# The first quad's layer-0 aggregation as seven block products, with the beginning in another order

## The chip, the cores and the metric

The kernel runs on one core of a Trainium2 chip. TensorE (PE) multiplies into PSUM, VectorE (DVE), ScalarE (ACT) and GpSimd (POOL) work on SBUF and PSUM, and SyncE (SP) issues every DMA of this kernel on one queue. The metric is the device time of one execution in microseconds: the median of three runs, 1771.18 us (1770.94 to 1771.25).

## The reference, cut to what matters

```python
# x: (16, 1024, 128) float32, adj: (1024, 1024) float32
h = relu(layernorm(x))                     # layer 0
x = x + (adj @ (h @ weight) + bias)
h = relu(layernorm(x))                     # layer 1: five gated steps
for _ in range(5):
    m = adj @ h                            # both matrices of the step are adj
    z = sigmoid(m @ w3 + h @ u3 + b3)      # w3 stands for the sum of its two halves
    r = sigmoid(m @ w4 + h @ u3 + b4)
    hv = tanh(m @ w5 + (r * h) @ u5 + b5)
    h = (1 - z) * h + z * hv
x = x + h
```

Everything is float32. Nearly all the arithmetic is `adj @ h`: once per batch in layer 0 and five times in layer 1.

## The kernel before, in words

The 16 batches are worked in four quads of four. One aggregation multiplies the adjacency matrix with the hidden states of a whole quad. In layer 1 it is done with Strassen's scheme in Winograd's form at two levels: seven big products, each again of seven small ones (`aggregate`, L502). The right operands of the small products are blocks of the transposed adjacency matrix and their sums and differences. They never change, so they are worked out once at the beginning (`right_sums`), written to DRAM tiles called `rd` (nine of the 49 stay in SBUF, `RESIDENT`), and read again for every aggregation in the fixed order `STREAM`, pair by pair, into `ring`, which has seven places for a pair (`stream`).

Layer 0 of the first two quads is done in the beginning, straight from the raw adjacency tiles. This document calls the aggregation of the first quad stage A and that of the second stage B.

- **Stage A** (`aggregate_plainly`, L549, names `pq_a0`): for each of two column halves of the adjacency matrix and each of four batches, eight matmuls of 128x128 by 128x512 into one PSUM bank, then a copy to `mT`. That is 64 matmuls.
- **Stage B** (`aggregate_by_seven`, L618, names `a_a1`, `b_a1`, `c_a1`): one level of the scheme. The left operand is a 2x2 matrix of blocks (two batches by two halves of the nodes), the right one the raw adjacency matrix in 2x2 blocks. Seven products p, each for two batches, each of four matmuls: 56 matmuls. Products 1, 2 and 3 take raw blocks; products 5, 6, 7 and 4 take differences T1, T2, T3 and T4 of raw blocks on the right, and sums S1 to S4 of the states on the left.
- After an aggregation, `po` (L741) multiplies `mT` with the layer's weight, four matmuls of 128x128 for each batch and half, and DVE adds the result to `x`.

The order is written out by hand. `pin` keeps each instruction in program order on its engine, so every engine is a queue. `put(k, ...)` hangs pieces on place k of the running aggregation, and `place(k)` issues them there, in the order in which they were put. In stage A before, k counts half rows of eight matmuls; in `aggregate_by_seven` k counts half-products (one product for one batch), 1 to 14.

Around the two stages lie these pieces:

- The loads. The adjacency matrix comes in eight tiles `raw[i][g]` of 512 KB (i: two chunks of 128 rows, g: column half). The g = 0 tiles lie in `big`, the others in `Z` and `little`. `x` comes in 512 KB a batch. `other_loads(k)` groups the loads behind the first ones; a memset of one column by DVE ahead of a group makes its first DMA wait until DVE has come that far, and SP, which issues in order, holds the rest.
- `Norm`, the layer norm of a batch: `bn_stats` (L330) on each of eight chunks, `bn_aggr` (L339), `ve` (L341) on DVE; the power -1/2 on POOL (L342, `rstd`); the shift on DVE (L347, `nmr`); eight `relu` activations on ACT (L360).
- The right sums. The big ones are T1 to T4, two differences of 128x1024 each, which lie in the ring's room until the ring is loaded for the first time. The small ones, for each of the seven big products in two halves: half 0 stores three blocks as they are and two computed ones, half 1 two more. Those in `RESIDENT` aren't stored. Each computed block is a 128x512 difference on DVE, and each store a DMA of 256 KB on SP's queue.
- In stage B, layer 1's input of the first quad is prepared: norm, `park` (four DMAs of 128 KB, `ft<-nat`), `store_x1` (one of 512 KB), then the load of the second quad's `x` into the same tile, and the transposing loads `sqt<-ft`. At its end stand seven `stream()` calls, which fill the ring for step 0, the first layer-1 aggregation.

Of the kernel before, what the change touches and what calls it, by code (L numbers as in the profile page):

```python
# [8 lines left out]
F32 = mybir.dt.float32  # L9
# [4 lines left out]
P = 128  # L14
# [82 lines left out]
def tile_two_gnn_layers(  # L97
# [36 lines left out]
    def x_tile(b):  # L134
        return pre.tile([P, NC, D], F32, tag="xt", name=f"xt_{b}")

    def load_x(b, xt=None, parts=((0, NC),)):
        xt = xt if xt is not None else x_tile(b)
        for cs in parts:
            cs = slice(*cs)  # L140
            dma(xt[:, cs], by_slots(x[b])[:, cs])
        return xt
# [23 lines left out]
    def flat(t):  # L166
        names = "abcd"[: len(t.shape) - 1]
        return t.rearrange(f"p {' '.join(names)} -> p ({' '.join(names)})")
# [7 lines left out]
    def load_adj(i, g):  # L176
        parts = SB if (i, g) == (0, 0) else 1
        for k in range(parts):
            cs = bass.ts(k, SB // parts)
            dma(raw[i][g][:, cs], adjT[:, bass.ts(i, SB), bass.ts(g, HALF)][:, cs])  # L180

    xts = {0: load_x(0, parts=((0, 2), (2, CH), (CH, NC)))}
    xts.update({b: x_tile(b) for b in range(1, Q)})
    for i in range(2):
        load_adj(i, 0)

    early_x = {}

    def other_loads(k):
        if k == 0:
            pin(nc.vector.memset(xts[1][:, 0, 0:1], 0.0))
            load_x(1, xts[1])
            load_adj(2, 0)
        elif k == 1:
            pin(nc.vector.memset(raw[3][0][:, 0, 0:1], 0.0))
            load_adj(3, 0)
        else:
            pin(nc.vector.memset(xts[2][:, 0, 0:1], 0.0))  # L200
            for b in range(2, Q):
                load_x(b, xts[b])
            for i in range(NB):
                load_adj(i, 1)
            for b in range(Q, Q + 3):
                early(b)
            dma(gb, gbias.to_broadcast([P, D]))
            dma(w_sb, weights)
            dma(b_sb, biases)
# [30 lines left out]

    def right_sums():

        rooms = [flat(ring[:, 4 * k : 4 * k + 4]) for k in range(3)]
        count = [0]

        def big_sum(n):
            room = rooms[{1: 2, 2: 0, 3: 1, 4: 2}[n]]
            T[n] = [room[:, bass.ts(k, N)].rearrange("p (c n) -> p c n", c=SB) for k in range(2)]
            for k in range(2):
                R = {(a, b): raw[2 * (a - 1) + k][b - 1] for a in (1, 2) for b in (1, 2)}  # L250
                a, b = {
                    1: (R[1, 2], R[1, 1]),
                    2: (R[2, 2], T.get(1, [0, 0])[k]),
                    3: (R[2, 2], R[1, 2]),
                    4: (R[2, 1], T.get(2, [0, 0])[k]),
                }[n]
                sub(T[n][k], a, b)

        def target(key):
            if key in RESIDENT:  # L260
# [23 lines left out]
                store_right((i, 4), t4)  # L284
                store_right((i, 7), t3)

        steps = [lambda n=n: big_sum(n) for n in (1, 2, 3)]
        steps += [lambda i=i, h=h: small_sums(i, h) for i in (3, 2, 0, 4, 1, 5) for h in range(2)]
        steps += [lambda: big_sum(4)]
        steps += [lambda h=h: small_sums(6, h) for h in range(2)]  # L290
        return steps

    streamed = [0]

# [243 lines left out]
                piece()  # L538
            place(k + 1)

    def aggregate_plainly(hN, nm, place):

        k = 0
        for g in range(NH):
            for i in range(Q):
                bank = ps_g.tile([P, HALF], F32, tag="pg", name=f"pq_{nm}_{i}_{g}")
                for c in range(NC):
                    pin(
                        nc.tensor.matmul(  # L549
                            bank,  # L550
                            hN[i][:, c, :],
                            raw[c // SB][g][:, c % SB],
                            start=c == 0,
                            stop=c == NC - 1,
                        )
                    )
                    if c == CH - 1:
                        k += 1
                        place(k)
                pin(nc.scalar.copy(mT[:, i, bass.ts(g, HALF)], bank))  # L560
                k += 1
                place(k)

    def aggregate_by_seven(hN, nm, place):

        S = {}
        for n in (2, 1, 3):
            t = flip.tile([P, 2, CH, D], F32, tag="sq", name=f"S{n}_{nm}")
            S[n] = [t[:, i] for i in range(2)]
        S[4] = []  # L570
        for i in range(2):
            t = work.tile([P, HALF], F32, tag="hv", name=f"S4{i}_{nm}", bufs=3)
            S[4].append(t.rearrange("p (j d) -> p j d", j=CH))

        def part(a, b, i):
            return hN[2 * a + i][:, bass.ts(b, CH)]

        def left_sums(n):
            for i in range(2):
                op, x, y = {  # L580
                    1: (add, part(1, 0, i), part(1, 1, i)),
                    2: (sub, S[1][i], part(0, 0, i)),
                    3: (sub, part(0, 0, i), part(1, 0, i)),
                    4: (sub, part(0, 1, i), S[2][i]),
                }[n]
                op(S[n][i], x, y)

        def result(a, b, i):
            return mT[:, 2 * a + i, bass.ts(b, HALF)]

        left_sums(1)
        left_sums(2)
        banks, fifth = {}, {}
        k = 0
        for p in BIG:
            right = big_right(BIG.index(p)) if p in (1, 2, 3) else T[{5: 1, 6: 2, 7: 3, 4: 4}[p]]
            for i in range(2):
                left = {
# [17 lines left out]
                for c in range(CH):  # L616
# [7 lines left out]
                            skip_group_check=True,  # L624
                        )
                    )
                if p == 2:
                    add(result(0, 0, i), bank, result(0, 0, i))
                elif p == 3:
                    add(result(0, 1, i), bank, result(0, 1, i))  # L630
                elif p == 5:
                    fifth[i] = work.tile([P, HALF], F32, tag="z", name=f"P5{i}_{nm}")
                    pin(nc.scalar.copy(fifth[i], bank))
                else:
                    o = {1: result(0, 0, i), 6: result(0, 1, i), 7: result(1, 1, i), 4: result(1, 0, i)}[p]
                    pin(nc.scalar.copy(o, bank))
                    if p == 7:
                        add(o, o, fifth[i])
                k += 1
                if k in (3, 4):  # L640
                    left_sums(k)
                place(k)


    def scratch_for(kind, nm):

# [465 lines left out]
    firsts = [slotwise(nat[:, k]) for k in range(Q)]  # L1112
    seconds = [slotwise(hT_all[:, 1, k].rearrange("p (a j e) -> p a j e", a=NSQ, e=SQ)) for k in range(Q)]

    one, two = Norm(xts[0], firsts[0][1], "a0"), Norm(xts[1], firsts[1][1], "a1")
    parts = (range(2), range(2, CH), range(CH, NC))
    for k in range(2):
        one.statistics(parts[k])
        one.scales(parts[k])
        if k == 0:  # L1120
            other_loads(0)
    one.shift(parts[0])
    one.relu(parts[0])
    one.statistics(parts[2])
    one.scales(parts[2])
    other_loads(1)
    one.shift(parts[1])
    one.relu(parts[1])
    one.shift(parts[2])
    one.relu(parts[2])  # L1130
    two.statistics(range(CH))
    other_loads(2)
    two.statistics(range(CH, NC))
    two.scales(EVERY)
    two.shift(EVERY)
    two.relu(EVERY)

    sums = right_sums()

# [1 line left out]
        for _ in range(n):  # L1141
            put(k, sums.pop(0))

    def norm_at(k, src, dst, nm, done=None, now=None):

        box = {}

        def begin():
            box["n"] = Norm(src(), dst, nm)
            box["n"].statistics(EVERY)  # L1150
            box["n"].scales(EVERY)

        def rest():
            box["n"].shift(EVERY)
            box["n"].relu(EVERY)
            if done:
                done()

        put(k, begin)
        if now is not None:  # L1160
            sums_at(k, now)
        put(k + 1 if now is None else k, rest)

    norm_at(1, lambda: xts[2], firsts[2][1], "a2")
    norm_at(2, lambda: xts[3], firsts[3][1], "a3", now=0)
    sums_at(3, 1)
    for b, k in zip(range(Q, 2 * Q), (4, 5, 6, 8)):
        done = (lambda: early(2 * Q - 1)) if b == Q else None
        norm_at(k, lambda b=b: early_x[b], seconds[b - Q][1], f"a{b}", done, 1)
    for b in range(Q):  # L1170
        put(8 + b, lambda b=b: bias(b))
    for k in (7, *range(9, 16)):
        sums_at(k, 1)
    for b in range(Q):
        put(11 + b, lambda b=b: po(b, 0))
    put(15, lambda: po(0, 1))
    put(16, lambda: po(1, 1))
    aggregate_plainly([s for s, _ in firsts], "a0", place)

    put(1, lambda: po(2, 1))  # L1180
    put(2, lambda: po(3, 1))

    def first_done(b):
        park(b, nat[:, b])
# [5 lines left out]
    for b in range(Q):  # L1190
        norm_at(2 * b + 1, lambda b=b: xts[b], nat[:, b], f"b{b}", lambda b=b: first_done(b))
        put((3, 5, 7, 10)[b], lambda b=b: xts.update({Q + b: load_x(Q + b)}))
        put((6, 8, 10, 14)[b], lambda b=b: bias(Q + b))
    for k in (2, 4, 8, 9, 10):
        sums_at(k, 1)
    put(7, weight_sums)
    for b, g, k in ((0, 0, 7), (1, 0, 9), (2, 1, 11), (0, 1, 13), (1, 1, 13), (3, 1, 14)):
# [5 lines left out]
    put(12, *early_0[2:6])  # L1203
    put(13, *early_0[6:8])
    put(14, *early_0[8:10])
    aggregate_by_seven([s for s, _ in seconds], "a1", place)
    for _ in range(RING // 2):
        stream()
    for b in range(2):
# [66 lines left out]
```

## Time and profile before

| what | value |
|---|---|
| median of three timed runs | 1771.18 us |
| span of the profiled execution | 1768.8 us |
| TensorE busy | 1759.3 us, 99% of the span |
| DVE busy | 1375.7 us |
| ACT busy | 899.0 us |
| mean granted TensorE clock | 0.999 |
| DMA moved | 396.88 MB, 224 GB/s over the span |
| stage A, first to last matmul's successor | 5.48 to 69.43 us |
| stage B, to the first product of step 0 | 69.43 to 126.43 us |

The page gives no other time for the profiled execution than its span; the timed runs' median is 2.4 us longer. In the lines of a timeline the first number is the start in microseconds from the span's start, the second the length of the merged group, then the engine, the line of the kernel, the operation, the tiles written and read, and the number of instructions; in brackets stands how long the engine was idle before, and what ended that wait. A line of a table by stretch gives the stretch, its length, the busy microseconds and instructions of PE, PEld (the weight load), DVE, ACT and POOL, then the granted clock, the mean busy share of the 16 DMA engines and the GB/s that they moved.

### The profile page before, as it was taken

The numbers are of one execution on the slowest core, as the hardware profiler recorded it, in microseconds if no ns is written. First come the engines' busy times: TensorE is split into PE (matmuls) and PEld (weight loads), VectorE is DVE, ScalarE is ACT, GpSimd is POOL, SyncE is SP. The second block draws the span as 40 slices with busy tenths as digits, with TensorE's granted clock in tenths as the row PEclk, the third lists the DMA queues.
The fourth block names the chain that finished last, engine by engine and source line by source line (L and its number), as shares of the span: only waits on it lengthen the run. The fifth ranks groups of instructions, "written<-read, shape, count | busy, mean of one in ns | idle before, by whom it ended". The sixth has DMA issues, their size and how long they took to land.

```text
span 1768.8 us, 21424 instructions
## 1 busy us (share of the span) xinstructions
PE 1759.3 (99%) x6438; PEld 1200.6 (68%) x6438; DVE 1375.7 (78%) x2806; ACT 899.0 (51%) x1974; POOL 59.0 (3%) x41
## 2 busy tenths in 40 slices
PE   9999999999999999999999999999999999999998
PEld 3557667589585775858857667585775857667584
DVE  6778988777878687887687968777687777868787
ACT  5246556544555555554455554545455454545544
POOL 3101000000000000000000000000000000000000
PEclk9999999999999999999999999999999999999999
DMA  7499786578595956749849577594866749476684
GB/s 258 157 324 306 235 257 214 179 240 250 129 305 185 284 198 195 236 135 284 241 146 326 176 227 279 153 295 158 247 210 194 252 135 294 164 232 225 197 279 173
DMA packets 169970, 396.88 MB, mean 224 GB/s; under 512 B 18560, under 2 KB 88064, under 8 KB 169856
## 3 DMA queue, kind: packets, MB, share of 16 engines
q1 hardware_dynamic: 169856, 395.52, 70.7%
q8 instruction: 52, 0.85, 0.2%
q14 instruction: 62, 0.51, 0.1%
HBM read 314.44 MB, written 81.00 MB: 224 GB/s over the span
## 4 chain that ended last, share of the span: by engine, by line
PE 95%; DVE 2%; POOL 1%; ACT 1%; DMA 1%; issue 0%; SPq 0%; DVEq 0%; POOLq 0%
PE a L502 27%; PE c L502 13%; PE b L502 7%; PE a_a L502 3%; PE pr_1A L806 2%; PE pr_3B L806 2%; PE pr_2B L806 2%; PE pr_0B L806 2%; PE pr_3A L806 2%; PE pr_2A L806 2%; PE pr_1B L806 2%; PE pr_0A L806 2%; PE pr_4B L806 2%; PE pr_4A L806 2%; PE a_a L618 2%; PE pv_0A L806 2%
## 5 line engine op out<-in xcount | busy, mean ns | idle before, releaser
L502 PE MATMUL a<-ring,big 128*128 128x256 f32 x1120 | 287.9, 379 | 0.3 <-ACT Z L521 0.3
L521 ACT COPY Z<-a 128x256 f32<-128x256 f32 x480 | 177.2, 371 | 192.8 <-PE a L502 192.6
L239 DVE TENSOR_TENSOR Z<-Z,taps 128x512 f32<-128x512 f32 (+1 forms) x264 | 144.8, 555 | 164.9 <-ACT taps L521 164.6
L502 PE MATMUL c<-ring,little 128*128 128x256 f32 x960 | 246.4, 379 | 0.0
L502 PEld LDWEIGHTS a<-ring,big 128*128 128x128 f32 x1120 | 212.2, 190 | 37.5 <-issue 8.1
L239 DVE TENSOR_TENSOR mT<-mT,Z 128x1024 f32<-128x1024 f32 x154 | 188.5, 1224 | 22.8 <-ACT Z L521 17.2
L502 PEld LDWEIGHTS c<-ring,little 128*128 128x128 f32 x960 | 182.2, 190 | 25.1 <-ACT taps L521 0.2
L521 ACT COPY taps<-c 128x256 f32<-128x256 f32 x280 | 103.7, 371 | 115.8 <-PE c L502 110.4
L502 PE MATMUL a<-resident,little 128*128 128x256 f32 x560 | 143.8, 379 | 0.0
L502 PE MATMUL a<-ring,little 128*128 128x256 f32 x560 | 143.7, 379 | 0.0
L502 PE MATMUL b<-ring,big 128*128 128x256 f32 x560 | 143.7, 379 | 0.0
L502 PEld LDWEIGHTS a<-resident,little 128*128 128x128 f32 x560 | 106.3, 190 | 14.7 <-ACT Z L521 0.3
L502 PEld LDWEIGHTS b<-ring,big 128*128 128x128 f32 x560 | 106.4, 190 | 14.5
L502 PEld LDWEIGHTS a<-ring,little 128*128 128x128 f32 x560 | 106.4, 190 | 14.5
L667 DVE STREAM_TRANSPOSE sq<-hT_all 128x512 f32<-128x512 f32 x152 | 98.6, 687 | 0.0
L239 DVE TENSOR_TENSOR little<-big 128x256 f32<-128x256 f32 x154 | 64.3, 418 | 21.5 <-ACT big L399 21.4
L399 ACT COPY big<-nat 128x512 f32<-128x512 f32 x132 | 80.7, 615 | 0.0
L521 ACT COPY taps<-b 128x256 f32<-128x256 f32 x140 | 52.1, 372 | 55.7 <-PE b L502 55.2
L236 DVE TENSOR_TENSOR little<-little,big 128x256 f32<-128x256 f32 x154 | 65.4, 425 | 6.7
L236 DVE TENSOR_TENSOR little<-big 128x256 f32<-128x256 f32 x154 | 64.4, 418 | 0.0
L236 DVE TENSOR_TENSOR little<-big,little 128x256 f32<-128x256 f32 x154 | 64.4, 418 | 0.0
L521 ACT COPY mT<-a 128x256 f32<-128x256 f32 x80 | 29.8, 373 | 48.3 <-PE a L502 48.3
(282 smaller groups left out, 2911.4 us busy)
## 6 DMA issues: line engine op xcount, KB each, us to landing
ring<-rd SPq DMA_DIRECT2D x440, 512.0 KB, 5.9
fn<-sq SPq DMA_DIRECT2D x76, 512.0 KB, 4.1
nat<-fn SPq DMA_DIRECT2D x256, 128.0 KB, 5.8
x1d<-xt SPq DMA_DIRECT2D x16, 512.0 KB, 5.6
sqt<-ft SPq DMA_DIRECT2D x16, 512.0 KB, 6.9
xt<-x1d SPq DMA_DIRECT2D x16, 512.0 KB, 7.5
xt<-in_x_dram SPq DMA_DIRECT2D x15, 512.0 KB, 4.8
out_dram<-xt SPq DMA_DIRECT2D x14, 512.0 KB, 6.7
```

Of the source, the lines that this page charges most:

```text
L236: pin(nc.vector.tensor_sub(o, a, b))
L239: pin(nc.vector.tensor_add(o, a, b))
L399: return [lambda i=i: pin(nc.scalar.copy(made_of(k, i), part(a, b, i))) for i in range(2)]
L502: nc.tensor.matmul(bank, l, right[:, c, :], start=opens and c == 0, stop=c == SB - 1, skip_group_check=True,)
L521: pin(nc.scalar.copy(to, bank))
L618: nc.tensor.matmul(bank, left[:, c, :], right[c // SB][:, c % SB], start=p in (1, 2, 5) and c == 0, stop=c == CH - 1, skip_group_check=True,)
L667: pin(nc.vector.transpose(squares_of_half(sq, g), transposed_half(hT, g)))
L806: nc.tensor.matmul(bank, w_sb[:, w, :], moving, start=start, stop=stop, skip_group_check=True)
```

## The change

Stage A is done by `aggregate_by_seven` too, with the products in the order 1, 2, 5, 6, 7, 3, 4 (stage B keeps 1, 2, 6, 5, 7, 3, 4). `aggregate_plainly` goes. The left sums become a function of their own (`sevens_left`), and their pieces are put at places; in stage A they lie in tiles of the hidden state that aren't in use yet. The two adds of product 2 in stage A are put at places 6 and 7.

The first loads and norms are reordered: the first halves of batches 0 and 1 come before their second halves, each with statistics of its own. The order of the later groups is batch 2, an adjacency tile and batch 3, then the four tiles with g = 1, then the rest.

T1, T2, T3 are put at places 3 to 8 of stage A as single halves, T4 at 10 and 11 (before: in stage B); T4 lies in the ring's last pair and in a tile of the hidden state. The small sums follow in the order 0, 1, 3, 2, 4, 5, 6 of the big products: four halves in stage A, ten in stage B (before: ten and four). Of the eight `po` of the first quad, six stay in stage A and two in stage B, but others than before.

```diff
-    xts = {0: load_x(0, parts=((0, 2), (2, CH), (CH, NC)))}
-    xts.update({b: x_tile(b) for b in range(1, Q)})
-    for i in range(2):
-        load_adj(i, 0)
+    xts = {b: x_tile(b) for b in range(Q)}
+    load_x(0, xts[0], ((0, 2), (2, CH)))
+    load_adj(0, 0)
+    load_x(1, xts[1], ((0, CH),))
+    load_adj(1, 0)
...
         if k == 0:
-            pin(nc.vector.memset(xts[1][:, 0, 0:1], 0.0))
-            load_x(1, xts[1])
+            mark(xts[0][:, CH, 0:1])
+            for b in range(2):
+                load_x(b, xts[b], ((CH, NC),))
             load_adj(2, 0)
         elif k == 1:
-            pin(nc.vector.memset(raw[3][0][:, 0, 0:1], 0.0))
+            mark(xts[2][:, 0, 0:1])
+            load_x(2, xts[2])
             load_adj(3, 0)
-        else:
-            pin(nc.vector.memset(xts[2][:, 0, 0:1], 0.0))
-            for b in range(2, Q):
-                load_x(b, xts[b])
+            load_x(3, xts[3])
+        elif k == 2:
+            mark(raw[0][1][:, 0, 0:1])
             for i in range(NB):
                 load_adj(i, 1)
+        else:
             for b in range(Q, Q + 3):
                 early(b)
...
-        steps = [lambda n=n: big_sum(n) for n in (1, 2, 3)]
-        steps += [lambda i=i, h=h: small_sums(i, h) for i in (3, 2, 0, 4, 1, 5) for h in range(2)]
-        steps += [lambda: big_sum(4)]
-        steps += [lambda h=h: small_sums(6, h) for h in range(2)]
-        return steps
+        return [lambda i=i, h=h: small_sums(i, h) for i in (0, 1, 3, 2, 4, 5, 6) for h in range(2)]
+
+    def big_sums(n):
+
+        rooms = [flat(ring[:, 4 * k : 4 * k + 4]) for k in range(3)]
+        if n == 4:
+            halves = [flat(ring[:, 12:14]), hT_all[:, 0, 3]]
...
+    one, two = norms[:2]
+    first, second = range(CH), range(CH, NC)
+    for part in (range(2), range(2, CH)):
+        one.statistics(part)
+        one.scales(part)
+    other_loads(0)
+    for part in (range(2), range(2, CH)):
+        one.shift(part)
+        one.relu(part)
+    two.statistics(first)
+    two.scales(first)
     other_loads(1)
+    one.statistics(second)
+    two.shift(first)
+    two.relu(first)
+    one.scales(second)
+    two.statistics(second)
+    one.shift(second)
+    one.relu(second)
+    two.scales(second)
     other_loads(2)
+    three, four = norms[2:]
+    three.statistics(EVERY)
+    two.shift(second)
+    two.relu(second)
+    three.scales(EVERY)
+    other_loads(3)
+
+    def span(n, k):
+        return [hT_all[:, 0, n].rearrange("p (i j d) -> p i j d", i=2, d=D)[:, i] for i in range(k)]
+
+    S = {1: span(0, 2), 2: span(1, 2), 3: span(0, 2), 4: span(2, 2)}
+    left = sevens_left([s for s, _ in firsts], S)
+    t1, t2, t3 = (big_sums(n) for n in (1, 2, 3))
...
+    put(
+        2,
+        lambda: four.statistics(first),
+        lambda: three.shift(EVERY),
+        lambda: three.relu(EVERY),
+        lambda: four.statistics(second),
+        lambda: four.scales(EVERY),
+    )
+    put(3, t1[0], lambda: four.shift(EVERY), lambda: four.relu(EVERY))
+    put(4, t1[1], left[1][0], left[2][0])
+    put(5, t2[0], left[1][1])
+    put(6, t2[1], left[2][1])
+    for b, k in zip(range(Q, 2 * Q), (7, 9, 11, 13)):
...
+    put(7, *left[3])
+    put(8, *t3)
+    put(9, *left[4])
+    put(10, lambda: put_t4(0))
+    put(11, lambda: put_t4(1))
...
+    for b, k in enumerate((9, 10, 12, 13)):
+        put(k, lambda b=b: bias(b))
+    for k in (10, 12, 13, 14):
         sums_at(k, 1)
+    for b, g, k in ((0, 0, 11), (1, 0, 12), (2, 1, 12), (0, 1, 13), (3, 1, 14), (1, 1, 14)):
+        put(k, lambda b=b, g=g: po(b, g))
+    late = {(2, 0): 6, (2, 1): 7}
+    aggregate_by_seven([s for s, _ in firsts], S, "a0", place, (1, 2, 5, 6, 7, 3, 4), late)
+
+    put(1, lambda: po(2, 0))
+    put(2, lambda: po(3, 0))
...
-    for k in (2, 4, 8, 9, 10):
+    for k in (2, 3, 4, 6, 7, 8, 9, 10, 12, 13):
         sums_at(k, 1)
```

## The prediction

> **What bounds the kernel now.** I read the head of the page, then TensorE in order of time over the first 130 us, then the DMA in stretches of the same time, because the diff touches only what runs there.
>
> ```profile
> span 1768.8 us, 21424 instructions
> PE 1759.3 (99%) x6438; PEld 1200.6 (68%) x6438; DVE 1375.7 (78%) x2806; ACT 899.0 (51%) x1974; POOL 59.0 (3%) x41
> PE 95%; DVE 2%; POOL 1%; ACT 1%; DMA 1%; issue 0%; SPq 0%; DVEq 0%; POOLq 0%
> ```
>
> TensorE is the bound over the whole span: any matmul that is removed is worth its full time, unless something else takes its place. From the timeline of TensorE:
>
> ```profile
> 8.88 1.96 PE L549 MATMUL pq_a<-big,nat 128*128 128x512 f32 x4 [1.06 <-ACT nat L360]
> 11.55 24.34 PE L549 MATMUL pq_a<-big,nat 128*128 128x512 f32 x56 [0.72 <-DMA big<-in_adjT_dram]
> 55.45 1.16 PE L741 MATMUL po<-w_sb,mT 128*128 128x128 f32 x8 [0.61 <-DVE xt L239]
> 69.43 3.60 PE L618 MATMUL a_a<-big,hT_all 128*128 128x512 f32 x8
> ```
>
> One matmul of the program is two records. The first quad's aggregation (stage A) runs from 5.48 to 69.43, with three gaps; the second quad's (stage B) starts at 69.43. In the chain of waits eight records of a 128x512 group advance 3.44 us, so a matmul costs 0.86 us, and a `po` (four of 128x128) 0.89. Stage B runs without a gap until the first product of step 0, at 126.43: 57.0 us. Now the DMA in stretches (busy microseconds per engine, clock, DMA share, GB/s):
>
> ```profile
> 50.00:64.00 14.00, 13.39 (x50) 7.28 (x49) 12.23 (x18) 1.38 (x3) 0.00 (x0) 1.00 0.98 351
> 84.00:92.00 8.00, 8.00 (x20) 3.60 (x19) 7.39 (x39) 3.65 (x9) 1.97 (x2) 1.00 0.92 306
> 108.00:116.00 8.00, 8.00 (x26) 3.98 (x25) 7.22 (x12) 1.21 (x3) 0.00 (x0) 1.00 1.09 368
> 116.00:124.00 8.00, 8.00 (x34) 4.65 (x33) 3.93 (x7) 1.68 (x4) 0.00 (x0) 1.00 0.99 390
> 84.00:122.00 38.00, 38.00 (x119) 19.29 (x118) 29.62 (x93) 15.39 (x35) 4.99 (x3) 1.00 0.93 307
> ```
>
> The last line is what decides here: once stage B's transfers begin, the DMA is 93% busy. They begin late; SP's queue shows the first store of stage B and the first load of the ring for step 0:
>
> ```profile
> 82.29 1.76 SPq L129 DMA_DIRECT2D ft<-nat  x4
> 115.75 14.65 SPq L129 DMA_DIRECT2D ring<-rd  x9
> ```
>
> The trace has the first ring pair landing at 123.75, only 2.7 us before its use at 126.43. Stage B is TensorE-bound by a margin of 2.7 us.
>
> **Stage A, part by part.** The seven products have 7 x 2 x 4 = 56 matmuls instead of 64: 8 x 0.86 = 6.9 us less, all on the path. Two gaps go too: the 0.72 (the third adjacency tile no longer comes second in line) and the 0.61 (`po` behind DVE; its place in the order changes). The 1.06 stays: chunk 2 of the first product still needs the second adjacency tile, which landed at 8.74 with as many bytes ahead of it as now. So -8.2 at most.
>
> What comes back is in the order of DVE, whose rows are: statistics of a batch 1.56, aggregation 0.55 (0.63 with its end), a 128x1024 difference 1.14, a 128x512 one 0.60 (pitch from start to start). The second half-product needs batch 1's first half. Its shift stands on DVE behind the statistics of batch 0's second half; that load lies 1.75 MB deep in the queue, where the old trace had about 9.4 us. Plus 0.8 for four statistics and 0.5 for the first relu: 10.8, where TensorE is ready at 10.84; I charge 0.35. Products 1 and 2 then end near 21.3. Product 5 needs T1 (two differences) and S1. In the new order stand: batch 3's statistics (its load 4 MB deep, about 15.1), its scales, T1[0], its shift, T1[1], S1[0]. From 15.1 that is 16.7 with batch 2's shift between, 18.3, 19.4, 20.3, 21.4, 22.0: a wait of 0.8 to 1.1. The shift waits for the `pow` on POOL, and its time varies with what DVE does:
>
> ```profile
> 21.64 1.64 POOL L342 TENSOR_TENSOR rstd_a<-ve_a,mhalf 128x8 f32<-128x8 f32 x1 [2.68 <-ACT nat L360]
> 28.23 2.45 POOL L342 TENSOR_TENSOR rstd_a<-ve_a,mhalf 128x8 f32<-128x8 f32 x1 [4.95 <-DVE ve_a L341]
> 38.48 1.92 POOL L342 TENSOR_TENSOR rstd_a<-ve_a,mhalf 128x8 f32<-128x8 f32 x1 [2.68 <-DVE ve_a L341]
> ```
>
> The 2.45 ran beside two 128x1024 differences, the 1.92 beside two of 128x512, the 1.64 beside an idle DVE. The new one runs beside one 128x1024: nearest to 1.92, so 0.3 more, and I take 1.4 for the wait. The ends are 0 (loads earlier) and 3 (loads 1 us later and a 2.45).
> [...]
>
> Stage A: -8.2 + 0.35 + 1.4 = -6.4; stage B starts near 63.0. Hidden in it:
> - DVE gets eight left sums and six result adds (14 x 0.60) and T4 (2 x 1.14) and gives six halves of small sums to stage B (12 x 0.60): +3.5 us, in a stage 6.4 us shorter. Between 20 and 70 DVE is idle 11.3 us (8.09, 8.75, 8.58, 9.89 and 3.40 busy in the ten-microsecond stretches). It fits with 1.4 to spare. Once that is gone, `po` and the first sums of stage B wait; the late p2 adds hold banks that nobody wants before stage B.
> - ScalarE copies ten half-products instead of eight: +1.1 us beside an engine 60 to 70% busy.
> - The marks (memsets of 0.06 us) gate loads behind DVE, and SP queues what follows. Each falls while 0.5 to 1 MB is still in flight, so no gap opens; the adjacency's second half lands near 20.5 instead of 22.4. Without that cover the price is one latency, 2.2 us (the first load's issue to landing), before T1.
> - Batches 4 to 7 are normalised at later places; the last relu ends about 1.5 us into stage B, whose first reader (S1) feeds the third product, 14 us in. T4's second half sits in the hidden-state tile that the last turn overwrites after stage B, as it does now.
>
> **Stage B and the ring.** This is the expensive move. Six halves of small sums go from A to B. They issue 17 stores of 0.262 MB, 4.46 MB, on SP's queue between parks, x1 stores and loads, ahead of the ring loads. DVE bears it (+7.3 for the sums, -2.3 for T4, on 41.9 busy of 57.0). The DMA has to move 38 x 0.307 = 11.7 MB as before plus 4.46 = 16.1 MB before the first ring pair. It cannot start earlier: SP has the first park in front, whose relu comes as long after stage B's start as now (first bytes 84.0 - 69.43 = 14.6 us in). Then:
> - at 390 GB/s, the best stretch: 41.4 us; pair lands 14.6 + 41.4 + 1.3 = 57.3 in, a wait of 0.3 beyond TensorE's 57.0;
> - at 307, stage B's own rate: 52.5 us; 68.4 in, a wait of 11.4;
> - at 351, the stretch of stores alone, and between the mixed 306 and 368: 46.0 us; 61.9 in, a wait of 4.9.
>
> I take 351: the gaps of the old stage B (7%) arise where SP waits for an x1 store before a load, and now there are stores in flight to fill them, but the mix with 1 KB-row parks keeps it below 390. [...]
>
> Step 0 afterwards does not add: in the old trace the ring's lead over TensorE grows from 2.7 to 9 us within nine pairs, since a pair lands every 1.3 us and lasts 1.7 or more.
>
> **Sum.** -6.4 + 4.9 = -1.5: step 0 starts at 124.9 instead of 126.4. The profiled span of 1768.8 becomes 1767.3; it stands 2.4 under the median of the timed runs (1771.18), which I take to stay: 1769.7.
>
> **The rivals.**
> 1. The DMA absorbs it (wait under 2.9 us): -6.4 + 0.3, 1765.1. For it: 390 GB/s where the queue was never empty, and the ring's 2.7 us of slack. Against it: parks and x loads in one queue ran at 306.
> 2. Slower, one mechanism: the 17 stores move at stage B's old rate, since SP still stands still for each x1 store before the load that reuses its tile. Step 0 starts 11.4 late: -6.4 + 11.4 = +5.0, 1776.2. It decides from a wait of 6.4 on (under 339 GB/s), and by more than the bound below from 9.9 (under 316). For it: the 307 and 0.93; against: the stores need no such wait.
> 3. DVE, not TensorE, sets stage A: the spare 1.4 us is too little, sums slip by 3 us, stage B starts at 66.0: the DMA chain moves with it, +1.5, 1772.7. For it: DVE busy 9.89 of 10 between 50 and 60; against: the 6.6 us idle after 60.
>
> **How the numbers follow.** About 0.2% (3.5 us) is what a measurement here can tell from no change. Forecast (wait 2.9 to 9.9): 0.50, and rival 3 at 0.07 on the same side, so within 0.2%: 0.57. Rival 1: 0.27, all faster. Rival 2: 0.16, slower by over 0.2% only in its upper part, but I count it whole, as a late DVE adds to it. Range: down to rival 1's 1765.1 less 0.3 for a wait of zero, up to 1775.0, which leaves out the worst of rival 2.
>
> **What would show it.** Right: stage B's first product near 63; one gap of about 1.4 us before product 5; 17 more stores between the parks; DMA share near 1.0 in stage B; and step 0's first product idle about 5 us for a ring load. Wrong: stage B later than 65 (a DVE step missed), no gap at step 0 (rival 1), or a gap over 10 us (rival 2).

## The result, and the profile after

The changed kernel takes 1777.18 us (median of six runs, 1776.31 to 1777.74) against 1771.75 of the kernel before (six runs beside it, 1770.94 to 1773.19): a ratio of 1.0032, 95% interval 1.0021 to 1.0042. It is slower by 0.3%. The forecast was 1769.7, within 0.2% of before, in a range of 1764.8 to 1775.0: time and sign both missed. The profiled execution took 1776.31, the fastest of the six. The head of its page:

```profile
span 1774.4 us, 21406 instructions
PE 1755.0 (99%) x6422; PEld 1199.8 (68%) x6422; DVE 1383.9 (78%) x2822; ACT 899.8 (51%) x1976; POOL 60.1 (3%) x42
```

TensorE has 16 records less, as the change says, and 4.3 us less busy time; the span is 5.6 us longer all the same. TensorE in order of time, over the beginning:

```profile
25.91 7.13 PE L598 MATMUL c_a<-ring,hT_all 128*128 128x512 f32 x16 [3.67 <-DVE hT_all L243]
65.71 3.60 PE L598 MATMUL a_a<-big,hT_all 128*128 128x512 f32 x8
117.66 1.16 PE L723 MATMUL po<-w_sb,mT 128*128 128x128 f32 x8 [1.79 <-DVE mT L243]
129.64 1.96 PE L510 MATMUL a<-ring,big 128*128 128x256 f32 x4 [4.70 <-DMA ring<-rd]
131.38 1.91 PE L510 MATMUL b<-ring,big 128*128 128x256 f32 x4
```

The brackets are what to read. Product 5 waits 3.67 for its left sum, so stage B starts at 65.71: 3.7 us earlier than before, not 6.4. In stage B a `po` waits 1.79, and step 0's first product waits 4.70 for the ring and starts at 129.64, 3.2 us later than before. And this product, two matmuls of 128x256 in four records, then advances 1.74 us instead of about 0.9: the clock. The `po` is late for the same reason as the ring: DVE, which it waits for, had itself stood idle for a load of `x` and for a transposing load, and with nine stores fewer in stage B (below) this wait is gone:

```profile
107.32 1.23 DVE L243 TENSOR_TENSOR xt<-xt,gb 128x1024 f32<-128x1024 f32 x1 [1.39 <-DMA xt<-in_x_dram]
112.33 1.30 DVE L681 STREAM_TRANSPOSE hT_all<-sqt 128x512 f32<-128x512 f32 x2 [1.38 <-DMA sqt<-ft]
```

Two stretches of the after trace, and the one of before that answers to the first of them (length, busy times by engine, granted clock, DMA share, GB/s):

```profile
80.28:129.59 49.31, 42.86 (x147) 22.77 (x145) 39.87 (x100) 15.88 (x36) 4.33 (x3) 1.00 1.01 343
129.79:133.20 3.41, 3.41 (x9) 2.70 (x10) 3.41 (x19) 0.37 (x1) 0.00 (x0) 0.50 1.03 418
```

```profile
84.00:123.75 39.75, 39.75 (x124) 20.05 (x122) 29.96 (x93) 15.39 (x35) 4.99 (x3) 1.00 0.93 312
```

Both begin 14.6 us into stage B, where its first bytes move, and end where the first ring pair lands. The DMA moved 49.31 us x 343 GB/s = 16.9 MB; before, 39.75 x 312 = 12.4 MB. The difference of 4.5 MB is the 17 stores. The DMA is full (1.01) for 49 us and TensorE has only 42.9 us of work beside it. Then the clock stands at 0.50 for 3.41 us.

The account, in the two profiled executions: stage B starts 3.72 earlier; it then takes 63.93 us to step 0's first product instead of 57.0 (+6.93: 4.70 for the ring, 1.79 for `po`, 0.44 in small change), so +3.21 there. The halved clock adds 1.7, and some small waits in step 0 of before (0.9 together) are gone: the same ScalarE copy of step 0 starts at 157.84 before and at 161.90 after, +4.06. That offset stays between 3.7 and 4.1 to 1721 us. The last 1.5 us come in the tail (1.05 around a wait for a ring load near 1726, 0.5 at the end). That wait stands in the profiles of two of the kernels below that share the changed beginning, and not in the others, so I do not count it to the change.

### The profile page after: what moved, and what is told of

Its sections match the earlier page's. It is cut to its first block, busy times and chain, and to the rows that moved or that the text cites. A ratio compares the mean times of both kernels' runs of the same rounds, so it can differ in the third digit from the quotient of the medians.

```text
span 1774.4 us, 21406 instructions
## 1 busy us (share of the span) xinstructions
PE 1755.0 (99%) x6422; PEld 1199.8 (68%) x6422; DVE 1383.9 (78%) x2822; ACT 899.8 (51%) x1976; POOL 60.1 (3%) x42
## 4 chain that ended last, share of the span: by engine, by line
PE 96%; DMA 2%; DVE 1%; SPq 0%; POOL 0%; issue 0%; ACT 0%; DVEq 0%; POOLq 0%
PE a L510 27%; PE c L510 13%; PE b L510 7%; PE a_a L510 3%; PE a_a L598 3%; PE pr_3B L788 2%; PE pr_2B L788 2%; PE pr_1B L788 2%; PE pr_0B L788 2%; PE pr_0A L788 2%; PE pr_3A L788 2%; PE pr_2A L788 2%; PE pr_1A L788 2%; PE pr_4B L788 2%; PE pr_4A L788 2%; PE c_a L598 2%
```

## The experiments

All of them against the kernel before, run beside them (medians of 1771.68, 1772.04 and 1771.82 in the three groups). The theory that the two profiles give: the 17 stores that moved to stage B stand ahead of the ring loads on a DMA that was nearly full (a share of 0.93 before, 1.01 after); the idle time that follows halves TensorE's clock; and stage A is late by its loads and by `pow` (the power -1/2 on POOL).

**One part alone: the six halves moved, in the kernel before.**

```diff
-        steps += [lambda i=i, h=h: small_sums(i, h) for i in (3, 2, 0, 4, 1, 5) for h in range(2)]
-        steps += [lambda: big_sum(4)]
+        steps += [lambda i=i, h=h: small_sums(i, h) for i in (0, 1, 3, 2, 4, 5) for h in range(2)]
+        steps.insert(-1, lambda: big_sum(4))
...
-    for k in (7, *range(9, 16)):
+    for k in (10, 13):
         sums_at(k, 1)
...
-    for k in (2, 4, 8, 9, 10):
+    for k in (2, 3, 4, 6, 7, 8, 9, 9, 10, 12, 13):
         sums_at(k, 1)
```

> The kernel before with one part of the change alone: six halves of small right operand sums (with their 17 stores) go from stage A to stage B; the first quad is aggregated plainly as before. Theory (the stores' bytes stand ahead of the ring loads on the DMA): stage B starts near 69.4 us as before, the first ring pair lands about 64 us into it as in the changed kernel, at 133.3 instead of 123.75, step 0's first product waits about 5 us or more and starts near 133, and the clock drops for 3.4 us afterwards (1.7 us): about 8 us slower than before, 1779 to 1780. Rival (the ring is late in the changed kernel for another reason, its loads or its DVE order in stage A, and the stores are hidden): step 0 starts at 126.4 to 128, 1771 to 1773.

Measured: 1779.75 us (1778.02 to 1783.65), ratio 1.0049 (1.0032 to 1.0066), 8 us slower than before. TensorE in order of time:

```profile
69.38 3.60 PE L618 MATMUL a_a<-big,hT_all 128*128 128x512 f32 x8
120.66 1.16 PE L741 MATMUL po<-w_sb,mT 128*128 128x128 f32 x8 [1.13 <-DVE mT L239]
133.51 2.08 PE L502 MATMUL a<-ring,big 128*128 128x256 f32 x4 [5.58 <-DMA ring<-rd]
```

Stage B starts where it did before, and the ring's wait appears, 64.1 us after stage B's start against 63.9 in the changed kernel; even the `po` behind DVE waits. The clock then stands at 0.50 for 6.83 us. The seven products have no part in it. This is the loss, isolated: the move alone costs 8 us, and the 3.7 us won in stage A paid back part of it.

**Nine of the 17 stores back in stage A, nothing else.** The stores of plain blocks (keys p = 1, 2, 3) need no sum on DVE, so they can be issued as soon as T1, T2 and T3 exist.

```diff
+    def store_blocks(i):
+        n = {5: 1, 6: 2, 7: 3, 4: 4}.get(BIG[i])
+        R = T[n] if n else big_right(i)
+        for p, (a, b) in ((1, (0, 0)), (2, (1, 0)), (3, (1, 1))):
+            store_right((i, p), R[a][:, :, bass.ts(b, BLK)])
...
-                for p, block in ((1, r[1, 1]), (2, r[2, 1]), (3, r[2, 2])):
-                    store_right((i, p), block)
+                if i not in (2, 3, 4):
+                    store_blocks(i)
...
+    for i, k in ((3, 6), (2, 8), (4, 10)):
+        put(k, lambda i=i: store_blocks(i))
```

> The changed kernel, but nine of the 17 stores, those of plain blocks of T1, T2 and T3 that need no sum on DVE, are issued in stage A at its sixth, eighth and tenth half-product instead of in stage B. Theory (bytes on the DMA): nine stores at 0.65 us each are 5.9 us less ahead of the ring, which lands near 123.7 instead of 129.6; the wait of 4.7 us shrinks to 0 to 1 and the clock's drop of 1.7 us is gone: 5 to 6.5 us faster than the changed kernel, 1770.7 to 1772.2. Rival (DVE's work of stage B or SP standing still for x loads sets when the ring is loaded): the ring lands at 128 to 130 all the same, 1776 to 1777.

Measured: 1771.04 us (ten runs, 1767.09 to 1771.94), ratio 0.9991 (0.9982 to 1.0001): 6.1 us faster than the changed kernel, inside the theory's 5 to 6.5. From the timeline of TensorE:

```profile
25.71 8.83 PE L604 MATMUL c_a<-ring,hT_all 128*128 128x512 f32 x16 [3.62 <-DVE hT_all L243]
67.20 3.60 PE L604 MATMUL a_a<-big,hT_all 128*128 128x512 f32 x8
125.67 1.13 PE L516 MATMUL a<-ring,big 128*128 128x256 f32 x4 [1.31 <-DMA ring<-rd]
```

The ring lands 58.4 us into stage B instead of 63.9, 5.5 earlier for nine stores, and no drop of the clock follows (1.00 in each stretch of 4 us from 122 to 142). The `po` that waited 1.79 no longer waits. DVE's work in stage B is what it was; bytes on the DMA set both waits. One line was unexpected: the wait of product 5 is the same as in the changed kernel, but its 16 records take 8.83 instead of 7.13 us. Here the clock halved in stage A: it is 0.50 from 25.94 to 29.35.

**The same bytes in another order: four ring loads earlier in the queue.**

```diff
+    put(11, stream, stream, stream, stream)
...
-    for _ in range(RING // 2):
+    for _ in range(RING // 2 - 4):
         stream()
```

> The changed kernel, with the same work and the same bytes, but four of the seven ring loads for step 0 are issued at the eleventh half-product of stage B, ahead of the last sums' stores, not after all of it. Theory (only the place in the queue makes the ring late): the first pair lands before 118, step 0's first product does not wait for it, the clock does not drop, and what is late next is a pair behind the fourth, by 0 to 2 us: 4 to 6.4 us faster than the changed kernel, 1770.8 to 1773. Rival (bytes alone count, and what is moved behind the ring, x and transposition loads, is waited for instead): po or step 0's normalisation waits 3 to 6 us, 1775 to 1778.

Measured: 1776.80 us (1774.39 to 1778.08), ratio 1.0026 (1.0016 to 1.0037): no gain that can be told from the changed kernel, as the rival had it.

```profile
126.75 1.13 PE L510 MATMUL a<-ring,big 128*128 128x256 f32 x4
137.18 1.10 PE L510 MATMUL a<-ring,little 128*128 128x256 f32 x4 [2.39 <-DMA ring<-rd]
145.37 1.13 PE L510 MATMUL a<-ring,big 128*128 128x256 f32 x4 [2.77 <-ACT Z L529]
```

The first product waits no more, but the fifth ring pair does, 10 us on, and a later wait of 2.77 follows. I had expected the first pair before 118; it was issued at 118.77 and landed at 126.71, since SP reached it late. On a DMA that was full here (shares of 1.00 to 1.08 from 122 to 138) the earlier place only moved the wait: 4.70 before the first pair became 2.39 before the fifth. In the 2.77 ScalarE stood behind the relus of one of layer 1's norms (`hb`), which had themselves waited 3.60 us for their shift on DVE.

**TensorE kept busy with unread matmuls before step 0.**

```diff
+    warm = ps_g.tile([P, HALF], F32, tag="pg", name="warm")
+    for _ in range(4):
+        pin(nc.tensor.matmul(warm, w_sb[:, 0, :], flat(w_sb[:, 0:4]), start=True, stop=True))
```

> The changed kernel with four matmuls of 128x512 whose result nobody reads, put between the last po of stage B and step 0's first product, that is into TensorE's idle 4.7 us. Theory (the idle stretch halves the clock for 3.4 us afterwards): the ring still lands near 129.6, the idle time shrinks to about 1.3 us, the clock stays at 1.0 after it, and the kernel is 1.7 us faster than the changed one: 1775.4. Rival (the clock's drop has another cause, or the first products of step 0 are slow for another reason): no change, 1777.

Measured: 1774.53 us (ten runs, 1771.76 to 1780.35), ratio 1.0017 (1.0007 to 1.0026): 2.7 us faster than the changed kernel, with 3.4 us more work on TensorE. The theory's sign is right and its 1.7 too small. The profiled run was the slowest of the ten and tells more than a typical one would. Its timeline of TensorE, and its clock in stretches:

```profile
25.55 9.86 PE L598 MATMUL c_a<-ring,hT_all 128*128 128x512 f32 x16 [3.55 <-DVE hT_all L243]
126.66 3.60 PE L1243 MATMUL warm<-w_sb 128*128 128x512 f32 x8
132.31 1.13 PE L510 MATMUL a<-ring,big 128*128 128x256 f32 x4 [2.06 <-DMA ring<-rd]
```

```profile
24.24:31.07 6.83, 5.52 (x7) 2.42 (x8) 6.79 (x13) 2.74 (x8) 0.00 (x0) 0.50 0.40 155
133.47:136.88 3.41, 3.41 (x9) 2.70 (x9) 2.32 (x18) 0.88 (x3) 0.88 (x1) 0.50 1.04 414
```

After product 5's wait the clock is 0.50 for 6.83 us (16 records in 9.86 instead of 7.13), and 2.06 us of idle time before step 0 were still enough to halve it once more. So this wait in stage A cost twice: 3.55 us as a wait and 2.73 as a slow clock. Of the five profiles in which product 5 waits 3.55 to 3.81 us, four show the drop (this one and the runs with nine stores moved, with four ring loads moved, and with the move undone); the changed kernel's own does not.

**T1 and S1 before batch 3's shift.**

```diff
-    put(3, t1[0], lambda: four.shift(EVERY), lambda: four.relu(EVERY))
-    put(4, t1[1], left[1][0], left[2][0])
+    put(3, *t1, left[1][0], lambda: four.shift(EVERY), lambda: four.relu(EVERY))
+    put(4, left[2][0])
```

The reason for it stands in the chain of waits of the changed kernel (start, length, what):

```profile
10.11 8.68 DMA xt<-in_x_dram
18.81 0.87 DVE stats_a L338 x4
19.76 0.79 DVE stats_a L338 x4
20.54 0.55 DVE mv_a L347 x8
21.46 2.48 POOL rstd_a L350
24.12 1.13 DVE ring L240
25.26 0.61 DVE hT_all L243
```

Batch 3's load of 8.68 us, the statistics, `pow` on POOL, and only behind its shift the second half of T1 (`ring`) and S1 (`hT_all`), which need no `pow` at all.

The chain names batch 3's load, but a second path through batch 2 ends at the same time here, and it is the one that counts:

```profile
15.29 1.64 DVE L338 BATCH_NORM_STATS2 stats_a<-xt 128x6 f32<-128x128 f32 x8 [2.27 <-DMA xt<-in_x_dram]
17.92 1.64 POOL L350 TENSOR_TENSOR rstd_a<-ve_a,mhalf 128x8 f32<-128x8 f32 x1 [3.82 <-ACT nat L368]
19.60 0.16 DVE L355 SCALAR_TENSOR_TENSOR nmr_a<-mv_a,rstd_a 128x8 f32<-128x8 f32 x1
```

Batch 2 lands at 15.26; its statistics, its `pow` and its shift stand on DVE ahead of the second half of batch 3's statistics (19.76). In each of the seven profiles with this order on DVE, product 5 starts 10.64 to 10.66 us after batch 2's landing, while batch 3 lands anywhere between 15.33 and 18.79.

> The changed kernel with one thing in another order on DVE in stage A: both halves of T1 and the first half of S1 come before the shift of batch 3 instead of around it. Theory (product 5 waits because that shift stands on DVE behind the 2.45 us of pow on POOL, and T1's second half and S1 stand behind the shift): product 5 starts near 24.2 instead of 25.9, its wait shrinks from 3.67 to about 2.0, stage B starts near 64.0, the clock halves less often after the wait; the ring's wait stays, since its transfers move along with stage B: 1.7 to 3.4 us faster than the changed kernel, 1773.8 to 1775.5. Rival (the loads set it): the second half-product of product 5 then waits for batch 3's relus for as long, 1776.5 to 1777.5.

Measured: 1774.23 us (ten runs, 1772.41 to 1777.92), ratio 1.0016 (1.0006 to 1.0025): 3.0 us faster than the changed kernel, as the theory had it.

```profile
23.74 3.70 PE L598 MATMUL c_a<-ring,hT_all 128*128 128x512 f32 x8 [1.83 <-DVE hT_all L243]
27.77 3.70 PE L598 MATMUL c_a<-ring,hT_all 128*128 128x512 f32 x8 [0.33 <-DVE hT_all L243]
64.13 3.60 PE L598 MATMUL a_a<-big,hT_all 128*128 128x512 f32 x8
127.20 2.07 PE L510 MATMUL a<-ring,big 128*128 128x256 f32 x4 [4.89 <-DMA ring<-rd]
```

The wait of 3.67 becomes 1.83 and 0.33. Counted from batch 2's landing (14.78 here), product 5 starts 8.96 us later instead of 10.65: 1.7 us is the new order, and 0.5 is a load that came earlier in this profile. The ring's wait stays, and step 0 moves forward with stage B: as long as the first store of stage B is timed by stage B's own norms, a gain in stage A reaches the end.

**Without the mark before batch 2's load.**

```diff
-            mark(xts[2][:, 0, 0:1])
             load_x(2, xts[2])
```

> The changed kernel without the mark (the memset on DVE) in front of batch 2's load, so that this load, the fourth adjacency tile and batch 3's load are issued as early as SP comes to them. Theory (the mark holds back issues, and batch 3 lands at 18.79 for it): batch 3 lands about 1 us earlier, product 5 starts up to 1 us earlier, 1776.2. Rival (the DMA is 91 to 95% busy from 6 to 18 us with or without the mark, and bytes set the landing; batch 0's and 1's second halves may land later): no change, 1776.5 to 1778.

Measured: 1773.85 us (ten runs, 1771.82 to 1775.39), ratio 1.0009 (0.9999 to 1.0018): 3.3 us faster than the changed kernel, three times what even the theory gave. The same stretch in the changed kernel and without the mark, and TensorE without it:

```profile
9.12:15.26 6.14, 5.89 (x13) 2.49 (x14) 2.88 (x23) 3.29 (x8) 3.02 (x3) 1.00 0.93 311
```

```profile
9.12:15.26 6.14, 6.06 (x15) 2.39 (x14) 5.22 (x39) 4.03 (x10) 2.43 (x3) 1.00 1.00 365
```

```profile
23.42 7.13 PE L597 MATMUL c_a<-ring,hT_all 128*128 128x512 f32 x16 [1.99 <-DVE hT_all L242]
63.21 3.60 PE L597 MATMUL a_a<-big,hT_all 128*128 128x512 f32 x8
126.30 2.07 PE L509 MATMUL a<-ring,big 128*128 128x256 f32 x4 [4.77 <-DMA ring<-rd]
```

With the mark, batch 2's load is issued at 9.26 and lands at 15.26; without it, it is issued at 6.33 and lands at 12.76, and batch 3 at 15.33 instead of 18.79. Product 5 starts 2.5 us earlier, which is what batch 2's load gained; batch 3's gained 3.5, more than product 5 did. A share of 0.93 had looked full. The GB/s show that it was not: 311 against 365.

**The move undone in the changed kernel.**

```diff
-    for k in (10, 12, 13, 14):
+    for k in (9, 10, 10, 11, 12, 12, 13, 13, 14, 14):
         sums_at(k, 1)
...
-    for k in (2, 3, 4, 6, 7, 8, 9, 10, 12, 13):
+    for k in (2, 4, 8, 9):
         sums_at(k, 1)
```

> The changed kernel with one part of the change undone: ten halves of small sums in stage A, as before the change, and four in stage B. Theory (the move of the sums and their stores is what the ring waits for, and DVE would not have borne them in stage A): the ring is in time, its wait of 4.7 and the clock's drop there are gone (-6.4), but DVE in stage A was idle for 3 us only between 27 and 66, and six halves at 1.2 us are 7.3, so stage B's first po and products start 3 to 4.5 us later: 1774 to 1775.5. Rival (DVE has room, the sums lie beside TensorE): the -6.4 stays, 1770 to 1771.5.

Measured: 1770.38 us (ten runs, 1767.73 to 1772.92), ratio 0.9992 (0.9982 to 1.0001): 6.8 us faster than the changed kernel. The rival wins: DVE bears the sums.

```profile
26.03 9.78 PE L598 MATMUL c_a<-ring,hT_all 128*128 128x512 f32 x16 [3.70 <-DVE hT_all L243]
58.35 1.16 PE L723 MATMUL po<-w_sb,mT 128*128 128x128 f32 x8 [0.15 <-DVE xt L243]
68.89 3.60 PE L598 MATMUL a_a<-big,hT_all 128*128 128x512 f32 x8
111.72 1.13 PE L723 MATMUL po<-w_sb,mT 128*128 128x128 f32 x8 [1.32 <-DVE mT L243]
127.63 1.13 PE L510 MATMUL a<-ring,big 128*128 128x256 f32 x4
```

DVE falls behind TensorE's program order in stage A, and one `po` waits 0.15 us for it; it catches up in stage B, where it has fewer sums. There another `po` waits 1.32 us, for a DVE that had itself stood idle 1.51 us for a transposing load. Stage B's later start, 68.89, is for the most part the halved clock of this profile (9.78 for product 5 instead of 7.13), not DVE. My count of idle time (3 us between 27 and 66) was no bound, since what is put at a place of stage A may run in stage B.

**Both cures, and more stores.** T1 and S1 first, as above, and the plain-block stores of the five sums 2 to 6 (15 stores) in stage A:

```diff
+    for i, k in ((5, 5), (3, 6), (2, 8), (4, 10), (6, 12)):
+        put(k, lambda i=i: store_blocks(i))
```

> The changed kernel with both cures: T1 and S1's first half before batch 3's shift, and the plain-block stores of five of the seven sums (15 stores, no work on DVE) issued in stage A at the half-products 5, 6, 8, 10 and 12. Theory: product 5 waits about 2.0, stage B starts near 64.0 to 65, the ring lands no later than TensorE needs it, no drop of the clock at step 0: 1767 to 1768.5, faster than both kernels. Rival (in a stage B with less in its way something else is late next, DVE's sums or the last x loads): 1769.5 to 1771.

Measured: 1766.77 us (seven runs, 1764.63 to 1767.45), ratio 0.9968 (0.9957 to 0.9979): faster than both kernels, 0.2 under the theory's range.

```profile
22.00 3.70 PE L604 MATMUL c_a<-ring,hT_all 128*128 128x512 f32 x8 [0.62 <-DVE hT_all L243]
62.39 3.60 PE L604 MATMUL a_a<-big,hT_all 128*128 128x512 f32 x8
120.38 1.13 PE L516 MATMUL a<-ring,big 128*128 128x256 f32 x4 [0.83 <-DMA ring<-rd]
```

In this profile the loads were also earlier, by 1.7 us or more, than in the seven others with the mark (`pow` of batch 3 starts at 19.23, against 20.97 to 22.08), so the 62.39 is partly luck.

**Unread matmuls in both waits of the changed kernel.** Besides the four before step 0, three in front of product 5:

```diff
+                if (nm, p, i) == ("a0", 5, 0):
+                    warm = ps_g.tile([P, HALF], F32, tag="pg", name="warm_a")
+                    for _ in range(3):
+                        pin(nc.tensor.matmul(warm, hN[0][:, 0, :], raw[0][0][:, 0], start=True, stop=True))
```

> The changed kernel with three unread 128x512 matmuls in front of product 5 in stage A, besides the four in front of step 0: TensorE's wait of 3.67 us there becomes about 1.1 us idle, product 5 starts when it did, and only the clock can gain. Theory (most runs of the changed kernel lose 1.7 us or more to a halved clock after that wait too, which the profiled one happened not to): 1.4 to 2.0 us under the median with step 0's matmuls alone (1774.53), 1772.5 to 1773.1, with a narrower spread. Rival (a wait of 3.6 us seldom halves the clock): 1774.5.

Measured: 1773.30 us (ten runs, 1772.33 to 1774.84), ratio 1.0008 (0.9999 to 1.0018).

```profile
21.97 2.74 PE L599 MATMUL warm_a<-big,nat 128*128 128x512 f32 x6
25.85 7.13 PE L602 MATMUL c_a<-ring,hT_all 128*128 128x512 f32 x16 [1.15 <-DVE hT_all L243]
128.38 1.13 PE L510 MATMUL a<-ring,big 128*128 128x256 f32 x4 [1.19 <-DMA ring<-rd]
```

Product 5 starts when it did (25.85) and step 0 when its ring lands; 6 us of useless matmuls make the kernel 3.9 us faster than the changed one, and 1.2 faster than with the four alone, a little less than the 1.4 to 2.0 expected. The spread of ten runs falls from 8.6 us (3.6 without the slowest one) to 2.5, and their mean clocks go from between 0.996 and 0.999 to between 0.998 and 1.000. This fits a variation between runs that comes from the clock; it does not show that all of it does.

**Both cures, without the mark.**

> The version with both cures (T1 and S1 before the shift, 15 plain-block stores in stage A), and without the mark in front of batch 2's load. Theory (without the mark batch 3 lands 3.5 us earlier, and product 5 then waits for nothing but its adjacency sums): product 5's wait of 0.6 to 1.8 goes, stage B starts near 62, the ring's wait stays under 2: 1765.5 to 1766.5, 0.3 to 1.3 under the version with the mark (1766.77). Rival (product 5 is ready no earlier because the loads of the adjacency's second half set T1, or the ring's transfers set step 0): 1766.5 to 1767.5.

Measured: 1764.40 us (five runs, 1764.02 to 1764.88), ratio 0.9958 (0.9945 to 0.9970): the lowest median, 7.4 us under before and 12.8 under the changed kernel, and 1.1 under the theory's range.

```profile
26.37 3.70 PE L603 MATMUL c_a<-ring,hT_all 128*128 128x512 f32 x8 [0.33 <-DVE hT_all L242]
62.73 3.60 PE L603 MATMUL a_a<-big,hT_all 128*128 128x512 f32 x8
121.54 1.13 PE L515 MATMUL a<-ring,big 128*128 128x256 f32 x4 [1.65 <-DMA ring<-rd]
```

The first half of product 5 waits for nothing. Stage B starts 6.7 us before the kernel before does, close to the 6.9 of the eight matmuls saved. What the mark is worth on top of the two cures these profiles do not show: batch 2 lands at 13.38 here and landed at 13.04 in the profile with the mark, and the intervals of the two ratios overlap.

## Why the prediction was wrong

The profiled span is 1774.4 us instead of 1767.3: about 2.7 more from stage A, 2.0 from stage B and 1.7 from the halved clock; the small waits that went (0.9) and the tail (1.5) make up the rest.

- **"-8.2 at most" in stage A**: right as far as it goes. With the waits cured, stage B starts 6.7 us earlier than before (62.73 against 69.43).
- **"Each falls while 0.5 to 1 MB is still in flight, so no gap opens" (the marks)**: failed, and it is the first cause in stage A. The mark before batch 2's load held its issue back from 6.33 to 9.26, the load landed at 15.26 instead of 12.76, and product 5 came 2.5 us later. Bytes were in flight, but they did not fill the DMA (311 GB/s against 365). The sum put this at nothing.
- **"From 15.1 that is 16.7 with batch 2's shift between" (the path to product 5)**: it starts at the wrong load. The path goes from batch 2's landing through two `pow` in a row, batch 2's and batch 3's. Without the mark batch 3 landed at 15.33, near the 15.1, and product 5 still started at 23.42 instead of 22.7 (21.3 and the wait of 1.4).
- **"Nearest to 1.92" (`pow`)**: mis-sized. It took 2.46 us in the changed kernel and 2.46 or 2.47 in six of the kernels built from it, those with T1 and S1 before the shift included: 0.5 above the term. In the changed kernel it ran beside one 128x1024 difference (T1's first half, from 21.20) and took what it had taken beside two in the old rows (2.45). The order of DVE mattered more than `pow`'s length: T1 and S1 stood behind the shift and needed nothing of it.
- **"I take 1.4 for the wait", ends 0 and 3**: 3.67, beyond the upper end. Product 5 started at 25.91 instead of 22.7: 2.5 of the 3.2 is the mark, the rest the path and `pow`; products 1 and 2 ended 0.9 later than taken (22.24), which hides that much of it. Stage B at 65.71 instead of 63.0. The text named a start after 65 as the sign of a missed step on DVE; it was mostly a missed step on SP's queue.
- **16.1 MB at 351 GB/s, 46.0 us**: mis-sized by 2.0. With the ring pair's own 0.5 MB and 1.3 us the forecast had 16.6 MB in 47.3 us; from the same start, 14.6 us into stage B, it was 16.9 MB at 343 GB/s = 49.3 us. The old bytes were counted over a stretch of 38 us that ended before the first pair landed (12.4 MB to 123.75, not 11.7 and 0.5), and the rate of a stretch of stores alone was too good for this mix. Together 63.9 us instead of 61.9. The mechanism was right: one kernel shows it with the move alone, another with nine stores taken back.
- **The wait of 4.9** came out as 4.70, but by two errors that cancel: the ring was 2.0 later, and TensorE too was later, by 1.79 for a `po` and 0.44 besides, which the forecast had not. "DVE bears it" counted DVE's work, which fits, and not its waits for loads on the same full DMA. Step 0 started at 129.64 instead of 124.9: 2.7 from stage A and 2.0 from stage B.
- **"Step 0 afterwards does not add"**: failed. It looked at the ring's lead and not at TensorE's clock, which had no term in the sum. The trace of before shows a drop only at its end (from 1765.99), where TensorE runs out of work. It cost 1.7 us at step 0 in the profiled run; in the other five runs the mean clock is 0.996 or 0.997 instead of 0.998, which would answer to one or two such drops more (an estimate: 3.41 us at half clock take 0.001 off the mean over 1774 us).
- **The rivals.** The second (slower, 1776.2) is nearest in time and names the right queue, but it decides by a wait of 11.4, and the wait was 4.7. The third has stage B at 66.0, near the 65.71, by a late DVE; DVE had room even for the sums that were moved away. None had two moderate delays and a clock that halved for 3.41 us behind one of them.
- **"It fits with 1.4 to spare"** (DVE in stage A) was read as a limit that six more halves would have broken. With the sums left in stage A, TensorE waited 0.15 us for DVE there, and 1.32 in stage B for a DVE that waited for a load. The move, the expensive part of the change, was not needed.

## What to carry to other kernels

Work that leaves a full engine takes its transfers with it (17 stores, 4.5 MB and 8 us here): before a step is moved, count the bytes that then stand ahead of the first load that somebody waits for, up to the moment when that load lands. A wait of an otherwise busy TensorE was charged twice here, once as idle time and once as a halved clock (4.70 us and then 1.7 in the changed kernel; 2.06 us of idle time was enough in one run), and where it stayed, matmuls that nobody reads were cheaper than silence (1774.53 and 1773.30 us against 1777.18). When several loads and engines end together, one chain of waits can name the wrong one: compare the distance from each load to the late product over several profiles. And the DMA that was 93% busy from 9.12 to 15.26 was not full (311 GB/s, against 365 without the mark): look at the GB/s, and at whether a load was held back by something that had nothing to do with it.

## What the runs showed of the hardware

In the changed kernel the granted clock is 0.50 for 3.41 us from 129.79, and again from 1771.60 on, when TensorE's last matmul is done. With four unread matmuls it is 0.50 for 6.83 us from 24.24, twice that, and for 3.41 from 133.47; with nine stores moved and with four ring loads earlier, for 3.41 in stage A (from 25.94 and from 27.30). The two starts in the changed kernel lie 1641.81 us apart, 481.0 times 3.4133, and those in the run with four unread matmuls 109.23, 32.0 times. So these traces can be cut into stretches of that length, counted from a drop, and TensorE's idle share counted in each.

| run | stretch | TensorE idle in it | clock in the next |
|---|---|---|---|
| changed kernel, product 5 | 20.57 to 23.98 | 1.74 us, 51% | 1.00 |
| changed kernel, product 5 | 23.98 to 27.39 | 1.93 us, 57% | 1.00 |
| changed kernel, step 0 | 126.38 to 129.79 | 3.26 us, 95% | 0.50 |
| changed kernel, step 0 | 129.79 to 133.20, at 0.50 | 0.00 us, 0% | 1.00 |
| changed kernel, last matmuls | 1768.19 to 1771.60 | 2.28 us, 67% | 0.50 |
| before, last matmuls | 1762.57 to 1765.99 | 2.05 us, 60% | 0.50 |
| four unread matmuls, product 5 | 20.83 to 24.24 | 2.24 us, 66% | 0.50 |
| four unread matmuls, product 5 | 24.24 to 27.65, at 0.50 | 1.31 us, 38% | 0.50 |
| four unread matmuls, step 0 | 130.06 to 133.47 | 2.06 us, 60% | 0.50 |

In the traces of before and of the changed kernel, from where the clock's record begins (at 4.71 and 6.91 us), no other stretch at full clock was idle for more than 1.52 us (45%), and none of those is followed by a drop. With four ring loads earlier, the stretch from 143.35, 34 lengths behind 27.30, holds 2.02 us (59%) of the wait of 2.77, and in the next one four records of 128x256 take 1.91 us instead of 1.03. So the 3.67 us at product 5, which fall into two stretches, did nothing in the profiled run of the changed kernel, while 3.55 in another run, and 2.06 at step 0 of that same run, halved the clock. Between 57% and 59% these runs show nothing.
